# A fixed vector-engine order, pairs of tiles and ScalarE roots in the opening stage of a graph layer

## The chip, the cores and the metric

The kernel runs on one core of a Trainium2 chip. The time is the device time of one execution in microseconds (us). Nine executions of the kernel before took 1905.69 to 1914.63 us, with a median of 1910.33 us. A separate execution was profiled; all lines of the profile come from that one.

In the profile, PE is TensorE's matmul unit and PEld its weight load, DVE is VectorE, ACT is ScalarE, POOL is GpSimd and SP is SyncE, which here only starts transfers. Each engine works through a queue of instructions in the order in which they stand there; a semaphore makes an instruction wait for another engine.

## The reference, cut to what matters

The layer normalises 3125 nodes of 256 features and sends the result through a graph network (GNN) and through a transformer with linear attention of depth 4; the sum of both goes through a mixture of experts.

```python
xn = _layernorm(x, axis=-1)
x = x + _L0_gnn_ref(xn, edge_attr_3, src, dst, ...) + _L0_mix_ref(xn[None], ...)[0]
x = x + _L0_ffn_ref(_layernorm(x, axis=-1)[None], ...)[0]
...
# in _L0_gnn_ref: 100000 edges
m = jnp.concatenate([h[edge_src], w], axis=1)
tmp = jax.nn.relu(m @ W1.T + b1)
h_N = jax.ops.segment_sum(tmp, edge_dst, num_segments=h.shape[0])
...
# in _L0_mix_ref, for each of 4 layers
h = _layernorm(x, ln1_g[i], ln1_b[i])
x = x + _linear_attn(h, Wq[i], Wk[i], Wv[i], Wo[i], bo[i])
h = _layernorm(x, ln2_g[i], ln2_b[i])
x = x + (jax.nn.gelu(h @ W1[i] + b1[i], approximate=False) @ W2[i] + b2[i])
...
# in _linear_attn, with 8 heads of 32
q = jax.nn.softmax(split(x @ Wq) * scale, axis=-1)
k = jax.nn.softmax(split(x @ Wk) * scale, axis=-2)
context = jnp.einsum('bhnd,bhne->bhde', k, v)
out = jnp.einsum('bhnd,bhde->bhne', q, context)
```

The part of the graph network that is the same for all edges of a source node, `xn @ W1[:, :256].T`, is computed once for each node; it is called `proj` here and lies in a table in DRAM, from which each edge gathers its row.

## The kernel before

The nodes stand in 25 tiles of 125 rows (partitions). Tiles are worked through in seven blocks (`BLOCKS`): five of four tiles, one of three, one of two. `pairs(b)` cuts a block into pairs of tiles, since two tiles of 256 columns fill one PSUM buffer of 512 columns; seven such buffers (`mm_tile`) go round.

The opening stage, which makes xn, proj and the attention inputs of layer 0, is a chain for each block b:

- `stage_xn` (L478 to L495): DVE takes the statistics of each tile (`bn_stats`, `bn_aggr`, L91 and L92) and from them two inverse roots for each row: that of the first normalisation and that of the second, which layer 0's attention applies to the normalised rows. Three small instructions (L488 to L490) make both arguments, `rsqrt` (L108 to L116) finds both roots at once by an integer first guess and three Newton steps, eleven small instructions. L493 normalises the tiles in place in `xm`, L495 makes the scale of the second normalisation.
- `stage_xnT`: PE transposes the normalised tiles (L238), ACT copies them out of PSUM (L509), SP stores them to DRAM for later (L510).
- `stage_xh1`: ACT multiplies by the second scale (L499).
- `stage_proj`: PE multiplies by `W1h` (L519), ACT copies (L521), SP writes the rows of the proj table.
- `stage_t1`: PE transposes the rows of `stage_xh1`, and ACT (L459) and DVE (L461), a half each, apply gain and bias: `hT`.
- `stage_k`: PE computes the k products of the block (L552), DVE takes their maximum over the nodes (L554), `neg` and, from block 1 on, `alpha` (L559, L567), ACT takes the exponentials (L563).
- `stage_q`: for each pair PE computes q products (L576), DVE takes the maximum of each head and subtracts it (L587, L588), ACT takes the exponentials (L589), DVE divides by the sum (L595 to L597).
- `stage_m`, `stage_ek`, `stage_qT`: the product of k and rows summed over nodes (L629, with DVE's L632 or L634), and transposes.

The loop over blocks (L817 to L844) does k, q of block b, m of block b-1, then xnT, xh1, proj and t1 of block b+1, then ek and qT of block b. `stage_xn(b + 2)` stands in it right after `stage_k(0, b)`. `windows` is a generator that prepares the sums of edges: it finds, from the sorted destinations `dst_i`, the first node of each strip of edges (DVE: L305, L308, L315, L319; two transposes on PE for each quarter, L314 and L318). The loop calls `next(prepared)` between its stages from block 2 on.

The order of work within an engine: `manual_schedule(engines=in_order)` (L808) keeps PE, ACT and POOL in the order of the program text. DVE isn't in that set in the opening stage: there a scheduler chooses DVE's order from its own estimates. Later, around `context` and `stage_y`, DVE is in program order as well (L848).

POOL clears the table `hNT` (two halves of 3157 columns) at the start, in one instruction (L273); the table collects the sums of messages, to which DVE adds windows from L370 on. POOL also makes the identity mask `ident`, which all transposes use, and starts the gathers of proj rows (L348), each group behind a tiny copy (`tick`, L436) that waits until a named tile is written.

Of the kernel before, what the change touches and what calls it, by code (L numbers as in the profile page):

```python
# [39 lines left out]
BT = 4  # L40
# [25 lines left out]
def gps_layer(ctx: ExitStack, tc: tile.TileContext, a, out):  # L66
    nc = tc.nc

    def cols(t0, n=1):
        return slice(t0 * TP, (t0 + n) * TP)  # L70
# [149 lines left out]
    with ExitStack() as ph:  # L220
# [49 lines left out]
        w1w = edge.tile([P, SC * D], F32, name="w1w", bufs=1)  # L270
        proj = dram.tile([N, D], F32, name="proj")
        xnT_d = dram.tile([P, KC, N], F32, name="xnT_d")
        nc.gpsimd.memset(hNT, 0.0)  # L273


        xv = by_tile(a["x"])
# [198 lines left out]

        def stage_xn(b):  # L478
            r = BLOCKS[b]
            n = len(r)  # L480
            for t in r:
                stats(tmp, xm[:, t, :], t)
            rs = tmp.tile([TP, 3, 2, BT], F32, name="rs", bufs=3)
            st["rs", b] = rs
            v = mv[:, r[0]:r[-1] + 1, 1]
            if n < BT:
                nc.vector.memset(rs[:, 0], 1.0)
            nc.vector.tensor_scalar(rs[:, 0, 0, :n], v, EPS, None, op0=ALU.add)  # L488
            nc.vector.scalar_tensor_tensor(rs[:, 0, 1, :n], rs[:, 0, 0, :n], EPS, v, op0=ALU.mult, op1=ALU.add)
            nc.vector.tensor_mul(rs[:, 0, 1, :n], rs[:, 0, 1, :n], rs[:, 0, 0, :n])  # L490
            rsqrt(rs[:, 1], rs[:, 0], rs[:, 2])
            for i, t in enumerate(r):
                nc.vector.tensor_scalar(xm[:, t, :], xm[:, t, :], mv[:, t, 0:1], rs[:, 1, 0, i:i + 1],  # L493
                                        op0=ALU.subtract, op1=ALU.mult)
            nc.vector.tensor_mul(rs[:, 2, 0, :], rs[:, 0, 0, :], rs[:, 1, 1, :])  # L495

        def stage_xh1(b):
            for i, t in enumerate(BLOCKS[b]):
                nc.scalar.activation(xh1s[b % 2][:, i, :D], xm[:, t, :], AF.Copy,  # L499
                                     scale=st["rs", b][:, 2, 0, i:i + 1])  # L500

        def stage_xnT(b):
            r = BLOCKS[b]
            xnT = stage0[:, b % 2 * KC * BT * TP:(b % 2 + 1) * KC * BT * TP].rearrange(
                "p (c m) -> p c m", c=KC)
            st["xnT", b] = xnT
            for t0, o, n in pairs(b):
                ps = transposed(xm[:, t0:t0 + n, :], n, "xnT_ps")
                nc.scalar.copy(xnT[:, :, cols(o, n)], ps)  # L509
            nc.sync.dma_start(xnT_d[:, :, cols(r[0], len(r))], xnT[:, :, :len(r) * TP])  # L510

        def stage_proj(b):
            r = BLOCKS[b]
            pj = pjs[b % 2]
            for t0, o, n in pairs(b):
                pp = mm_tile("proj_ps")[:TP].rearrange("p (i d) -> p i d", d=D)
                for i in range(n):
                    for c in range(KC):
                        nc.tensor.matmul(pp[:, i, :], st["xnT", b][:, c, cols(o + i)], w1h[:, c, :],  # L519
                                         start=(c == 0), stop=(c == KC - 1))  # L520
                nc.scalar.copy(pj[:, o:o + n, :], pp[:, :n, :])  # L521
            by_parts(nc.sync, by_tile(proj)[:, r[0]:r[-1] + 1, :], pj[:, :len(r), :])


        def stage_stats(b):
# [7 lines left out]
            for i, t in enumerate(r):  # L533
                normalize(xh1[:, i, :D], xm[:, t, :], t)

        def stage_t1(l, b):
            hT = tmp.tile([P, KC, BT * TP], F32, tag="hT", name="hT", bufs=2)
            st["hT", b] = hT
            for t0, o, n in pairs(b):
                ps = transposed(xh1s[b % 2][:, o:o + n, :D], n, "hT_ps")  # L540
                affine(hT[:, :, cols(o, n)], ps, l, 0)
                worked(n * KC * P, hT[:1, 1, o * TP:o * TP + 1])
# [55 lines left out]

        def stage_q(l, b):
            st["qs", b] = tmp.tile([TP, BT, D], F32, name="qs")  # L600
            for pair in pairs(b):
                qf, qm = q_exp(b, pair, q_products(b, pair))
                q_shares(pair, qf)
                worked(pair[2] * KC * D, qm[:1, :1])
# [203 lines left out]
        with tc.manual_schedule(engines=in_order):  # L808

            prepared = windows()  # L810
            stage_xn(0)
            stage_xnT(0)
            stage_xh1(0)
            stage_proj(0)
            stage_xn(1)
            stage_t1(0, 0)
            for b in range(NB):  # L817
                stage_k(0, b)
                if b + 2 < NB:
                    stage_xn(b + 2)  # L820
                if b < NB - 1:
                    stage_q(0, b)
                else:
                    held = True
                if b > 1:
                    next(prepared, None)
                if b > 0:
                    stage_m(0, b - 1)
                if b + 1 < NB:
                    stage_xnT(b + 1)  # L830
                    stage_xh1(b + 1)
                    if b > 1:
                        next(prepared, None)
                    stage_proj(b + 1)
                    stage_t1(0, b + 1)
                if b > 1:
                    next(prepared, None)
                stage_ek(0, b)
                if b < NB - 2:
                    stage_qT(0, b)  # L840
                if b == NB - 2:
                    for _ in prepared:
                        pass
                    spread = True  # L844
            stage_m(0, NB - 1)
            for l in range(last):
                start_layer(l)
                with tc.manual_schedule(engines={mybir.EngineType.DVE}):  # L848
                    if l == 0:
                        context(l, [lambda: stage_qT(l, NB - 2, slice(0, 1)),  # L850
                                    lambda: stage_qT(l, NB - 2, slice(1, 2)), lambda: None])
                    else:
                        context(l, [lambda: None, lambda: None, rest])
                    load(l + 1, "Wk", "Wq", "Wv")
                    (y00, y01), (y10, y11), (y20, y21) = [pairs(b) for b in range(3)]
                    y_added(*y_products(y00))
                    held, only_loads = False, True
                    y_added(*y_products(y01))
                    stage_ln2(0, None)
                    y10, y11 = y_products(y10), y_products(y11)  # L860
                    stage_qT(l, NB - 1)
                    y20 = y_products(y20)
                    y_added(*y10)
                    stage_t2(l, 0)
                    y21 = y_products(y21)
                    for y in (y11, y20, y21):
                        y_added(*y)
                    only_loads = False
                for b in range(NB):
                    stage_f1(l, b)  # L870
                    if b == 0:
                        add_b2(b)
                    if b > 1:
                        stage_ek(l + 1, b - 2)
                        stage_qT(l + 1, b - 2)
                    if 1 < b < NB - 1:
                        stage_y(l, b + 1)
                    if b > 1:
                        stage_m(l + 1, b - 2)
                    if b > 0:  # L880
                        stage_t1(l + 1, b - 1)
                    if b + 1 < NB:
                        stage_ln2(b + 1)
                    stage_f2(l, b)
                    stage_stats(b)
                    if b == NB - 1:
                        stage_ln1(b)
                        held = True
                        fill(2)
                    if b > 0:  # L890
                        stage_k(l + 1, b - 1)
                    if b + 1 < NB:
                        stage_t2(l, b + 1)
                    if b > 0:
                        stage_q(l + 1, b - 1)
                    if b < NB - 1:
                        stage_ln1(b)
                stage_ek(l + 1, NB - 2)
                stage_t1(l + 1, NB - 1)
                stage_m(l + 1, NB - 2, [0])  # L900
                stage_k(l + 1, NB - 1)
                stage_m(l + 1, NB - 2, [1])
                stage_qT(l + 1, NB - 2)
                stage_ek(l + 1, NB - 1)
                rest = fill_win()
                if l + 1 == last:
                    rest()
                stage_m(l + 1, NB - 1)
            while due:
                _, _, step, i = due.pop()  # L910
                step(i)
# [586 lines left out]
```

## Time and profile before

| what | value |
|---|---|
| median of nine executions | 1910.33 us |
| the profiled execution: its time | 1907.14 us |
| the profiled execution: its span | 1905.4 us |
| PE busy, 0 to 20 us and 20 to 40 us | 9.63 us, 14.06 us |
| PE busy, 40 to 60, 60 to 80, 80 to 100, 100 to 120 us | 19.76, 19.87, 19.84, 19.66 us |
| granted clock of PE, whole span | 0.976 |
| first k product of block 0, 1, 2, 3, 4 | 18.96, 43.85, 61.54, 79.34, 97.25 us |
| first gather of proj rows | 132.56 us |

Times within the execution count from the start of its span. The span leaves out what lies around it (1.7 us here). A row of the timeline holds the start, the length, the engine, the line, the operation, the tile that is written and those that are read, their sizes, the number of instructions merged, and, in square brackets, how long the engine had been idle and what released it. The granted clock is the share of its full clock that PE was given.

The opening stage in the order of PE's work: block 0's transposes begin at 9.63 us and its proj at 11.46; the k products of block 0 begin at 18.96, wait 3.62 us for the second half of `hT` and go on from 23.68; block 1's proj begins at 36.02. From about 40 us on PE has no gaps of more than 0.3 us until block 3's end.

### The profile page before, as it was taken

The numbers are of one execution on the slowest core, as the hardware profiler recorded it, in microseconds if no ns is written. First come the engines' busy times: TensorE is split into PE (matmuls) and PEld (weight loads), VectorE is DVE, ScalarE is ACT, GpSimd is POOL, SyncE is SP. The second block draws the span as 40 slices with busy tenths as digits, with TensorE's granted clock in tenths as the row PEclk, the third lists the DMA queues.
The fourth block names the chain that finished last, engine by engine and source line by source line (L and its number), as shares of the span: only waits on it lengthen the run. The fifth ranks groups of instructions, "written<-read, shape, count | busy, mean of one in ns | idle before, by whom it ended". The sixth has DMA issues, their size and how long they took to land. (4 is left out here: it accounts for less than half of the span.)

```text
span 1905.4 us, 28580 instructions
## 1 busy us (share of the span) xinstructions
PE 1796.4 (94%) x8965; PEld 1217.4 (64%) x8965; DVE 1161.6 (61%) x3729; ACT 746.0 (39%) x1352; POOL 1110.2 (58%) x1404
## 2 busy tenths in 40 slices
PE   6999899999989999999899999999999999999975
PEld 4875555666655565566665656656677777788752
DVE  8656576756774666666666667666555665433326
ACT  3543354444524544554334445444222222222213
POOL 1006788788828888888468788881123337555521
PEclk8999999999989999999999999999999998999997
DMA  6212333333523333334323333332221004677836
GB/s 164 95 63 81 95 110 100 99 103 103 152 67 92 103 101 102 109 103 128 114 68 107 95 105 103 104 105 76 86 70 31 20 17 123 209 277 269 282 121 196
DMA packets 95089, 216.64 MB, mean 114 GB/s; under 512 B 26761, under 2 KB 53392, under 8 KB 90193
## 3 DMA queue, kind: packets, MB, share of 16 engines
q0 software_dynamic: 45904, 121.36, 22.3%
q1 hardware_dynamic: 49024, 93.34, 15.4%
q8 instruction: 77, 1.26, 0.3%
q14 instruction: 84, 0.68, 0.1%
HBM read 192.20 MB, written 22.35 MB: 113 GB/s over the span
## 5 line engine op out<-in xcount | busy, mean ns | idle before, releaser
L348 POOL DMA_INDIRECT gat<-proj,src_i x784 | 760.4, 970 | 192.4 <-issue 144.9
L735 PE MATMUL f_ps<-h2T,ww 128*128 128x500 f32 (+2 forms) x896 | 360.6, 550 | 6.9 <-ACT h2T L459 6.2
L745 PE MATMUL f_ps<-ww,gT 128*125 128x256 f32 x1600 | 363.3, 382 | 0.0
L398 ACT ACTIVATE gat<-gat 128x512 f32<-128x512 f32 x392 | 238.6, 630 | 305.2 <-DVE gat L397 299.5
L397 DVE TENSOR_TENSOR gat<-gat,pw 128x512 f32<-128x512 f32 x392 | 250.3, 677 | 160.8 <-PE pw L392 141.3
L745 PEld LDWEIGHTS f_ps<-ww,gT 128*125 128x125 f32 x1600 | 294.1, 188 | 70.4 <-issue 18.2
L735 PEld LDWEIGHTS f_ps<-h2T,ww 128*128 128x128 f32 x896 | 166.5, 192 | 178.7 <-issue 125.9
L737 ACT ACTIVATE gT<-f_ps,ffb 128x500 f32<-128x500 f32 (+2 forms) x224 | 135.3, 631 | 134.9 <-PE f_ps L735 134.6
L378 PE MATMUL pq<-gat,hot 128*32 128x256 f32 x1568 | 131.5, 390 | 10.1 <-ACT gat L398 8.8
L370 DVE TENSOR_TENSOR hNT<-hNT,win_ps 128x64 f32 x392 | 84.5, 215 | 64.9 <-PE win_ps L367 54.4
L392 PE MATMUL pw<-w1w,ea 8*128 8x512 f32 x784 | 119.3, 639 | 0.5 <-ACT gT L737 0.3
L750 DVE TENSOR_TENSOR xm<-xm,f_ps 125x512 f32<-125x512 f32 (+1 forms) x52 | 34.7, 667 | 138.0 <-PE f_ps L745 130.6
L1201 POOL DMA_INDIRECT slots<-rec,at x50 | 59.4, 1189 | 101.0 <-DVE rs_u L115 63.8
L576 PE MATMUL q_ps<-wwq,hT 128*125 128x256 f32 x400 | 97.1, 394 | 6.8 <-DVE gat L397 5.0
L629 PE MATMUL m_ps<-xh,ek 125*128 125x257 f32 x400 | 95.6, 389 | 5.7 <-ACT ek L615 5.7
L211 POOL DMA_INDIRECT outs<-o,ids x50 | 49.3, 986 | 87.9 <-DVE o L209 86.9
L552 PE MATMUL k_ps<-hT,wwk 128*128 128x500 f32 (+2 forms) x224 | 94.6, 566 | 4.4 <-DVE hT L461 3.6
L204 PE MATMUL e_ps<-ew,hs 128*128 128x256 f32 x400 | 97.2, 380 | 0.5 <-DVE o L208 0.3
L688 PE MATMUL y_ps<-mo,qT 128*125 128x256 f32 x400 | 92.6, 382 | 3.4 <-DVE mo L678 3.4
L576 PEld LDWEIGHTS q_ps<-wwq,hT 128*125 128x125 f32 x400 | 75.8, 194 | 28.4 <-DVE gat L397 8.6
L91 DVE BATCH_NORM_STATS2 bnst<-xm 125x6 f32<-125x256 f32 x225 | 89.6, 413 | 4.6 <-DMA xm<-x 2.4
L629 PEld LDWEIGHTS m_ps<-xh,ek 125*128 125x128 f32 x400 | 76.2, 194 | 20.3 <-ACT ek L615 7.2
(270 smaller groups left out, 2546.1 us busy)
## 6 DMA issues: line engine op xcount, KB each, us to landing
ew<-ffn_w SPq DMA_DIRECT2D x33, 1154.0 KB
gat<-proj,src_i POOLq DMA_INDIRECT x784
ww<-mix_W SPq DMA_DIRECT2D x8, 1024.0 KB
ea<-ea_g SPq DMA_DIRECT2D x98, 64.0 KB
hNT<-ffn_w SPq DMA_DIRECT2D x4, 1154.0 KB
ogs<-outs SPq DMA_DIRECT2D x10, 448.0 KB
xnT_d<-stage SPq DMA_DIRECT2D x5, 500.0 KB
xnT<-xnT_d SPq DMA_DIRECT2D x5, 500.0 KB
```

Source lines behind the costliest of these rows:

```text
L204: nc.tensor.matmul(ps[:, j, :], x["hs"][:, f, j * P:(j + 1) * P], x["w2"][:, f, :], start=(f == 0), stop=(f == NEF - 1))
L348: nc.gpsimd.indirect_dma_start(out=gats[-1][:, (j // SC) % 2, j % SC, :], out_offset=None, in_=proj, in_offset=bass.IndirectOffsetOnAxis(a ...
L378: nc.tensor.matmul(pq[s * W:(s + 1) * W, :], hot[:, s * SC + i, :], gats[s // 2][:, s % 2, i, :], start=(i == 0), stop=(i == SC - 1))
L392: nc.tensor.matmul(pws[s], ea[s * W:s * W + SC * 4, :], w1w[s * W:s * W + SC * 4, :], start=True, stop=True)
L397: nc.vector.tensor_add(msg, msg, pws[s])
L398: nc.scalar.activation(msg, msg, AF.Relu)
L552: nc.tensor.matmul(ps, wt["Wk"][:, h, c * P:(c + 1) * P], hT[:, h, :m], start=(h == 0), stop=(h == KC - 1))
L576: nc.tensor.matmul(ps[:, i, :], st["hT", b][:, c, cols(o + i)], wt["Wq"][:, c, :], start=(c == 0), stop=(c == KC - 1))
L629: nc.tensor.matmul(ps, st["ek", b][:, i, c * P:(c + 1) * P], xh1s[b % 2][:, i, :], start=(i == 0), stop=(i == n - 1))
L735: nc.tensor.matmul(ps, wt["W1"][:, c, f * P:(f + 1) * P], st["h2T", b][:, c, :m], start=(c == 0), stop=(c == KC - 1))
L737: nc.scalar.activation(gT[:, f, :m], ps, AF.Gelu, bias=ffb[:, l, f:f + 1])
L745: nc.tensor.matmul(ps[:, i, :], st["gT", b][:, f, cols(o + i)], wt["W2"][:, f, :], start=(f == 0), stop=(f == NF - 1))
```

## The change

DVE joins the engines in program order from the start of the opening stage to its end (`prologue`). The stages of block 0, and `stage_xn` of block 1, are cut into pairs of tiles, and the calls for the pairs are interleaved by hand. For these two blocks ACT's `Sqrt` and DVE's `reciprocal` take the place of the integer guess and Newton steps; all other blocks keep `rsqrt`. In layer 0, `stage_q` does products, subtraction and exponential of both pairs first, and then the divisions of both. The clearing of `hNT` is cut into four pieces, each on POOL behind a tick on `hT` of blocks 1 to 4.

```diff
-        nc.gpsimd.memset(hNT, 0.0)
...
-        def stage_xn(b):
+        def stage_xn(b, part=None):
+
             r = BLOCKS[b]
-            n = len(r)
-            for t in r:
+            o, n = (0, len(r)) if part is None else pairs(b)[part][1:]
+            tt = slice(r[0] + o, r[0] + o + n)
+            for t in range(tt.start, tt.stop):
                 stats(tmp, xm[:, t, :], t)
...
-            rsqrt(rs[:, 1], rs[:, 0], rs[:, 2])
...
+            v, rv, ru, rw = mv[:, tt, 1], *[rs[:, k, :, o:o + n] for k in range(3)]
+            nc.vector.tensor_scalar(rv[:, 0], v, EPS, None, op0=ALU.add)
+            nc.vector.scalar_tensor_tensor(rv[:, 1], rv[:, 0], EPS, v, op0=ALU.mult, op1=ALU.add)
+            nc.vector.tensor_mul(rv[:, 1], rv[:, 1], rv[:, 0])
+            if part is None:
+                rsqrt(ru, rv, rw)
+            else:
+                nc.scalar.activation(rw, rv, AF.Sqrt)
+                nc.vector.reciprocal(ru, rw)
...
         def stage_q(l, b):
             st["qs", b] = tmp.tile([TP, BT, D], F32, name="qs")
+            if l == 0:
+                for pair, qf in [(pair, q_exp(b, pair, q_products(b, pair))[0]) for pair in pairs(b)]:
+                    q_shares(pair, qf)
+                return
...
             prepared = windows()
-            stage_xn(0)
-            stage_xnT(0)
-            stage_xh1(0)
-            stage_proj(0)
-            stage_xn(1)
-            stage_t1(0, 0)
+            prologue = ExitStack()
+            prologue.enter_context(tc.manual_schedule(engines={mybir.EngineType.DVE}))
+            one, two = slice(0, 1), slice(1, None)
+            stage_xn(0, 0)
+            stage_xnT(0, one)
+            stage_xn(0, 1)
+            stage_xh1(0, one)
+            stage_proj(0, one)
+            stage_xnT(0, two)
+            stage_xn(1, 0)
+            stage_t1(0, 0, one)
+            stage_xh1(0, two)
+            stage_proj(0, two)
+            stage_t1(0, 0, two)
+            stage_xn(1, 1)
             for b in range(NB):
                 stage_k(0, b)
                 if b + 2 < NB:
...
                     stage_proj(b + 1)
                     stage_t1(0, b + 1)
+                    if b < 4:
+                        nc.gpsimd.tensor_copy(tick, st["hT", b + 1][:1, 0, :1])
+                        nc.gpsimd.memset(hNT[:, b % 2, b // 2 * N // 2:(b // 2 + 1) * N // 2 + b // 2 * W], 0.0)
...
             stage_m(0, NB - 1)
+            prologue.close()
```

`stage_xnT`, `stage_xh1`, `stage_proj` and `stage_t1` take the pair as an argument, too; the transfers of `stage_xnT` and `stage_proj` are issued once, with a block's last pair.

## The prediction

> **What bounds the kernel now.** I read the busy shares first, then stretches of 20 us, then the order of time from 10 to 80 us, then the granted clock in steps of 1 us.
>
> ```profile
> PE 1796.4 (94%) x8965; PEld 1217.4 (64%) x8965; DVE 1161.6 (61%) x3729; ACT 746.0 (39%) x1352; POOL 1110.2 (58%) x1404
> ...
> 20.00:40.00 20.00, 14.06 (x42) 9.40 (x42) 17.32 (x74) 5.57 (x11) 0.00 (x0) 0.74 0.35 111
> ...
> 60.00:80.00 20.00, 19.87 (x108) 16.08 (x107) 14.77 (x47) 11.55 (x25) 0.00 (x0) 1.00 0.23 77
> ```
>
> PE is busy 94% of the span, so time is won only where PE stands still or slow. Columns of a stretch: length, then busy us of PE, PEld, DVE, ACT, POOL, then the granted clock. From 0 to 40 us PE works 23.7 us, so up to 16 us are open. From 40 us on, in the attention blocks of layer 0, PE is full: blocks 1 to 3 start their k products at 43.85, 61.54, 79.34 us, 17.7 us apart. There a new wait costs its full length. One such block, start and length in us:
>
> ```profile
> 61.54 3.52 PE L552 MATMUL k_ps<-hT,wwk 128*128 128x500 f32 x8
> ...
> 66.08 0.15 DVE L567 TENSOR_TENSOR alpha<-kmax,kmax 128x2 f32<-128x2 f32 x1
> ...
> 66.83 0.69 DVE L587 TENSOR_REDUCE qm<-q_ps 125x16 f32<-125x512 f32 x1 [0.59 <-PE q_ps L576]
> ...
> 69.75 0.68 DVE L588 TENSOR_TENSOR qs<-q_ps,qm 125x512 f32<-125x512 f32 x1
> ...
> 70.47 0.63 ACT L589 ACTIVATE qs<-qs 125x512 f32<-125x512 f32 x1 [1.50 <-DVE qs L588]
> ...
> 72.46 1.05 ACT L509 COPY stage<-xnT_ps 128x500 f32<-128x500 f32 x2 [1.36 <-PE xnT_ps L238]
> ...
> 73.09 3.72 PE L519 MATMUL proj_ps<-w1h,stage 128*125 128x256 f32 x16
> ```
>
> The reader is to see a chain: DVE's second subtract of q (69.75) releases ACT's second exp; ACT, in a fixed order, copies xnT only behind it; PE's proj needs that copy. Here ACT waits 1.36 us for PE, so the chain has that much slack. It has it because DVE, whose order a scheduler chose, goes from alpha straight to q; the normalisation of block b+2 was done in idle DVE time before.
>
> **The change, part by part.** All is summed on the profiled span (1905.4 us; that execution took 1907.14; the median shown is 1910.33, 4.9 above the span) and the difference is added to the median.
>
> *Clearing hNT.* One POOL memset of 5.36 us (6314 columns) becomes four of 1562 or 1595 columns, by columns 1.33 to 1.35 us each, each behind a 0.18 us tick. POOL is idle 124.7 us before its tick at 131.45, and DVE first adds to hNT at 178.07: cost 0. Were that cover gone, 6 us would lie before the first gather (132.56). The next write of hT in that buffer must wait for the tick, two blocks later: 0. The identity mask, behind the memset at 6.37, is free about 5 us sooner, which the earlier transposes below need.
>
> *Block 0 in pairs, roots on ACT.* The Newton steps L110 to L116 are 11 instructions 0.20 us apart, 2.2 us; a Sqrt and a reciprocal take their place, by the nearest small rows (ACT alpha 0.20, DVE reciprocal 0.24) 0.5 us with hand-over. Two tiles: statistics from 4.00 to 5.15, three small ops to 5.72, root and reciprocal to 6.2, tile 0 normalised at 6.6. PE starts there, 3.0 us before the 9.63 of now. From there ACT's and PE's orders decide: proj of the first pair, at the slow 0.46 us per matmul that the first eight show now (3.7 us), from 8.45 to 12.15; the second pair's copy to 13.7; block 1's first root stands behind that copy, so DVE idles from 11.8 to 13.95; proj of the second pair ends 16.3 (2.15 us, as the second eight now) to 17.8 (slow again); the last half of hT is written at 18.0 to 19.6, against 23.63 now. Block 1's second half then takes DVE 3.0 us, the two k reductions and neg 1.5: neg at 22.5 to 24.0, against 29.85 now. So 6 to 7 us are won here. Block 0's DMAs (three) are the same; SP now issues an ea load and a 1 MB weight ahead of block 1's proj, which only the gather at 132.56 waits for: 0.
>
> The Trainium skill (ScalarE: Activation LUTs, What ACT_TABLE_LOAD costs) asks about 2.7 us for each change of table set and tells to do all of one set first, which speaks against roots in a kernel of exps. In this trace a load takes 1283 ns. The built order has one more load, behind the last root and ahead of the first exp, where ACT waits some 2 us for neg anyway: 0 by the row; by the page at most 0.7 us.
>
> *DVE in program order.* Now neg is followed by all of stage_xn(b+2), and only then by q. Its price: statistics in strict alternation as in layer 0's y stage, 0.56 us per tile and 0.64 for the last (148.55, 149.11, 149.75), 2.32; from L488 to the next stage 12.27 to 16.45, 4.18; together 6.5 us for four tiles. These rows are of the same instructions:
>
> ```profile
> 12.27 0.17 DVE L488 TENSOR_SCALAR rs<-mv 125x4 f32<-125x4 f32 x1
> ...
> 15.08 1.38 DVE L493 TENSOR_SCALAR xm<-xm,mv,rs 125x256 f32<-125x256 f32 x4
> ...
> 16.38 0.15 DVE L495 TENSOR_TENSOR rs<-rs 125x4 f32<-125x4 f32 x1
> 16.45 0.74 DVE L91 BATCH_NORM_STATS2 bnst<-xm 125x6 f32<-125x256 f32 x2
> ```
>
> Queued behind it on DVE is q, behind q's exps on ACT the copy of xnT(b+1), behind that PE's proj. Block 1, in us from its k: alpha 4.54, xn 4.62 to 11.1; maximum, subtract, maximum, subtract start 11.1, 11.82, 12.42, 13.14 (0.72 and 0.60 apart as in the rows; both subtracts now come before the sums, which saves 0.88 against now), the last ends 13.82; exp to 14.49; copy, 0.63 later proj at 15.1 where it now is at 11.55: **+3.55**. PE has finished m and xnT at 11.3 and idles 3.8.
> Block 2: the first part of the windows (L305 0.56, L308 0.96), which the scheduler had put at 21.15, now follows the last share of q (16.30): done at 18.5. PE's least transpose stands between xnT and proj and waits for it: proj at 18.6, **+7.05**.
> Block 3: three tiles (5.7 us), last share at 15.5, then lcol, for which PE's base transpose waits ahead of proj: 16.6 for 11.66, **+4.9**.
> Block 4: two tiles (4.8 us), proj at 13.4 for 11.66, **+1.7**. Blocks 5 and 6 have no such stage: 0. Sum 17.2 us.
> Block 0 likewise: from neg, xn(2) and q hold proj(1) until 32.9 to 34.4, against 36.02. So of the 6 to 7 us only 1.6 to 3.1 reach proj(1).
>
> *The clock.* An idle PE is followed by slow matmuls (length, PE busy, granted clock, DMA share, GB/s):
>
> ```profile
> 21.00:22.00 1.00, 0.00 (x0) 1.00 0.57 172
> 22.00:23.00 1.00, 0.00 (x0) 0.88 0.22 41
> 23.00:24.00 1.00, 0.32 (x1) 0.50 0.49 134
> ...
> 29.00:30.00 1.00, 1.00 (x5) 0.70 0.00 0
> ```
>
> Three stalls of now: 3.6 us before 23.68, then 6.0 us at half clock; 2.3 us before 36.02, 3.4 us; 5.5 us before 202.47, 4.7 us. Half of that is lost: 3.0, 1.7, 2.4, mean 2.4. Blocks 1 to 3 idle 3.8, 7.2 and 5.0 us: 2.4 each, 7.2 together, bounds 0 and 3 x 3.0 = 9. Block 4 idles 1.9, less than any of the three: 0 (1.7 as a bound). Block 0's stall, 7 us, pays 2.4 too, where now it pays 1.7: k(1) comes 0.9 to 2.4 earlier, taken 1.7.
> The Trainium skill (TensorE: Matmul & The Clock Gate, What's actually happening) gives free-running windows of about 3.4 us: one idle window halves the clock, a busy one restores it. The drops here last about 3.4 and 6.8 us, as it says, but the 2.3 us gap also dropped the clock, which its "at least one idle window" would spare; by the page alone block 1's stall would drop it only where it meets a window whole, and the sum would be about 2 us lower.
>
> *After the prologue* DVE's scheduler orders block 1 of the first feed-forward a little differently. PE waits 5.46 us there for a gather that POOL, saturated since 149 us, issues; that shifts with everything else: 0, bounds -2.4 and +2.4 (one clock drop).
>
> **Sum:** 17.2 + 7.2 - 1.7 = +22.7 us; on the median 1933.0. Least: 17.2 + 0 - 2.4 - 2.4 = +12.4, 1923; most: 17.2 + 9 + 1.7 + 2.4 - 0.9 = +29.4, 1940.
>
> **The rivals.**
> *The stalls come, the clock holds.* +15.5, 1926. For it: at 142 to 144 us PE was idle 1.9 us and the clock stayed 1.00. Against: the three drops above. It lies inside my bounds.
> *DVE keeps up; faster.* One mechanism: DVE gets through xn(b+2) so quickly that q's second subtract ends by 10.3 us after k (8.9 now, plus the slack of 1.36), so that ACT again waits for PE. That takes a stage of 3.0 us instead of 6.5. There it is about even: proj(1) at 29.6 to 31.1 wins 4.9 to 6.4, and the windows' ops in blocks 2 and 3 still cost 3.5 and 1.4. It decides below 3.0; with 1.0 us block 0 wins 7.7 and block 2 loses 1.5, -6.2: 1904. For it: the small ops are busy only 0.17 of 0.20 us. Against: the four L493 alone take 1.38 and four statistics 1.5.
> *The edit isn't what it says:* in the built programs DVE stands in program order up to block 5, so this falls.
> *Worse:* clock drops as long as the 10 us from 1606 to 1616, and the scheduler's new order costs too: +35, 1945.
>
> **How the numbers follow.** Forecast with its clock variants 0.80, its own range 1923 to 1940; faster 0.11; a stage near the 3.0 us, that is no change, 0.03; worse 0.06. About 0.2% (3.8 us) is what can be told from no change here. The range goes down to 1917 for a stall partly hidden and to 1942. Faster 0.11, same 0.03, slower 0.86.
>
> **What would show it.** Right: k(0)'s neg near 23 us; ACT's xnT copies behind a wait for DVE's qs instead of PE; PE idle 3 to 7 us ahead of proj in blocks 1, 2 and 3, the longest in block 2 at the least transpose; these blocks 23 to 28 us long; clock 0.5 in them. Wrong: blocks still 17.7 us apart, or a first block that saves over 10 us at k(1).

## The result, and the profile after

The changed kernel is slower: 1928.39 us (median of 13 executions, 1923.37 to 1934.38) against 1910.28 us (40 executions of the kernel before); the ratio is 1.0101, 95% interval 1.0090 to 1.0111. Its profiled span is 1931.5 us, granted clock 0.97, against 1905.4 and 0.976. Chips differ: the kernel before takes 1903.7 to 1904.7 us on those of nine runs below, and 2164.5 us, at a granted clock of 0.923 to 0.935, on that of three (Newton steps, the table cleared first, q in pairs alone). So each run is given as a ratio to the kernel before on its own chip, and of those three only the first 120 us of the trace are compared.

The table compares k products, at which blocks begin (us from the start of the span). Below, k(1) is the first k product of block 1, and so on; mo is the product of the output weights and the context, which follows the attention blocks of a layer.

| first k product of block | 0 | 1 | 2 | 3 | 4 | 5 |
|---|---|---|---|---|---|---|
| before | 18.96 | 43.85 | 61.54 | 79.34 | 97.25 | 114.08 |
| after | 16.28 | 39.50 | 62.30 | 89.98 | 114.70 | 133.15 |
| difference | -2.68 | -4.35 | +0.76 | +10.64 | +17.45 | +19.07 |

Block 0 wins 4.35 us; blocks 1 to 4 lose 5.11, 9.88, 6.81 and 1.62. At the first mo product +18.4 us is left of it, close to the difference of the medians (18.1). First the busy shares of the changed kernel's page, then its stretches (length, busy us of PE, PEld, DVE, ACT, POOL, granted clock, DMA share, GB/s):

```profile
PE 1804.4 (93%) x8965; PEld 1223.0 (63%) x8965; DVE 1170.1 (61%) x3719; ACT 748.2 (39%) x1357; POOL 1114.1 (58%) x1411
...
60.00:80.00 20.00, 13.61 (x71) 10.58 (x69) 14.85 (x46) 8.46 (x18) 1.62 (x3) 0.91 0.14 49
...
100.00:120.00 20.00, 15.01 (x70) 11.47 (x69) 10.59 (x27) 8.45 (x17) 1.54 (x2) 0.83 0.15 52
```

Over the span PE's share hardly moves, 94 to 93%; in the stretch from 60 to 80 us PE works 13.61 us where it worked 19.87. Block 2 in order of time, from the timelines of PE, DVE and ACT (start, length, engine; in brackets the idle time before and what ended it):

```profile
62.30 3.52 PE L563 MATMUL k_ps<-hT,wwk 128*128 128x500 f32 x8
...
66.91 0.42 DVE L91 BATCH_NORM_STATS2 bnst<-xm 125x6 f32<-125x256 f32 x1
...
73.28 0.15 DVE L502 TENSOR_TENSOR rs<-rs 125x4 f32<-125x4 f32 x1
...
75.39 0.69 DVE L599 TENSOR_TENSOR qs<-q_ps,qm 125x512 f32<-125x512 f32 x1
...
76.11 0.63 ACT L600 ACTIVATE qs<-qs 125x512 f32<-125x512 f32 x1 [0.63 <-DVE qs L599]
76.65 1.03 ACT L517 COPY stage<-xnT_ps 128x500 f32<-128x500 f32 x2
...
79.81 0.97 DVE L307 TENSOR_REDUCE least<-drel 128x392 f32<-128x784 f32 x1
...
80.92 0.42 PE L313 MATMUL least_ps<-ident,least 128*98 128x128 f32 x1 [7.32 <-DVE least L307]
81.14 6.31 PE L528 MATMUL proj_ps<-w1h,stage 128*125 128x256 f32 x16
```

From 66.91 to 73.35 us DVE does all of `stage_xn(4)`; only then q, whose second subtract ends at 76.1 us; ACT's copy of xnT follows the second exp without a gap, where before it waited 1.36 us for PE. The windows' minimum (79.81) is later still, and PE's small transpose needs it: idle for 7.32 us. Then proj takes 6.31 us instead of 3.72. The waits of PE up to 140 us, in total, number and longest:

```profile
PE proj_ps L528 <- ACT stage L517: 13.8, 5, 7.2
PE least_ps L313 <- DVE least L307: 7.3, 1, 7.3
...
PE base_ps L317 <- DVE lcol L314: 5.0, 1, 5.0
```

### The profile page after: what moved, and what is told of

The parts are those of the page before. It is cut to its first block, busy times and chain, and to the rows that moved or that the text cites. A ratio compares the mean times of both kernels' runs of the same rounds, so it can differ in the third digit from the quotient of the medians.

```text
span 1931.5 us, 28587 instructions
## 1 busy us (share of the span) xinstructions
PE 1804.4 (93%) x8965; PEld 1223.0 (63%) x8965; DVE 1170.1 (61%) x3719; ACT 748.2 (39%) x1357; POOL 1114.1 (58%) x1411
## 5 line engine op out<-in xcount | busy, mean ns | idle before, releaser
L760 PEld LDWEIGHTS f_ps<-ww,gT 128*125 128x125 f32 x1600 | 293.8, 188 | 71.3 <-issue 18.4
L703 PEld LDWEIGHTS y_ps<-mo,qT 128*125 128x125 f32 x400 | 75.1, 193 | 21.8 <-DVE mo L693 5.0
```

Source lines behind the costliest of these rows:

```text
L703: nc.tensor.matmul(ps[:, i, :], qT[:, c, cols(t0 + i)], mo[:, c, :], start=(c == 0), stop=(c == KC - 1))
L760: nc.tensor.matmul(ps[:, i, :], st["gT", b][:, f, cols(o + i)], wt["W2"][:, f, :], start=(f == 0), stop=(f == NF - 1))
```

## Experiments

First a table of all runs, with the length of each block in us, from its first k product to the next block's; then the single ones.

| run | block 0 | 1 | 2 | 3 | 4 | ratio to before |
|---|---|---|---|---|---|---|
| before | 24.89 | 17.69 | 17.80 | 17.91 | 16.83 | 1 |
| after | 23.22 | 22.80 | 27.68 | 24.72 | 18.45 | 1.0101 (1.0090 to 1.0111) |
| loop left to the scheduler | 15.88 | 17.94 | 18.76 | 17.98 | 16.84 | 0.9963 (0.9950 to 0.9975) |
| fixed order alone | 26.28 | 25.21 | 29.50 | 27.33 | 23.32 | 1.0165 (1.0151 to 1.0178) |
| after, xn behind q | 15.85 | 23.20 | 19.23 | 18.21 | 18.39 | 0.9998 (0.9987 to 1.0009) |
| after, long fillers | 24.10 | 23.67 | 30.79 | 27.17 | 20.12 | 1.0161 (1.0148 to 1.0174) |
| after, short fillers | 24.08 | 21.11 | 24.89 | 22.72 | 20.11 | 1.0071 (1.0057 to 1.0086) |
| after, windows early | 24.03 | 23.88 | 24.01 | 24.73 | 18.45 | 1.0081 (1.0067 to 1.0094) |
| after, q as before | 26.50 | 25.16 | 29.49 | 27.31 | 23.30 | 1.0160 (1.0146 to 1.0174) |
| after, no fixed order | 16.73 | 17.69 | 19.46 | 17.98 | 16.83 | 0.9991 (0.9981 to 1.0000) |
| loop free, Newton roots | 16.96 | 17.69 | 18.76 | 17.98 | 16.84 | 0.9994 (0.9971 to 1.0017) |
| loop free, table cleared first | 17.53 | 17.69 | 17.80 | 17.91 | 16.84 | 0.9972 (0.9938 to 1.0005) |
| before, q in pairs | 23.19 | 17.70 | 17.80 | 17.91 | 16.83 | 0.9989 (0.9963 to 1.0014) |
| loop free, pieces late | 15.87 | 17.69 | 17.81 | 17.90 | 16.84 | 0.9956 (0.9942 to 0.9969) |

### The loop left to the scheduler

```diff
             stage_xn(1, 1)
+            prologue.close()
             for b in range(NB):
...
             stage_m(0, NB - 1)
-            prologue.close()
```

> The changed kernel, but DVE is in fixed order only up to the last call ahead of the loop over blocks; inside the loop the scheduler orders it again. Theory (the loss is xn(b+2) standing ahead of q in the fixed order, and the pairs, roots and pieces by themselves help or cost nothing): the four stalls of 3.7, 7.3, 5.0 and 1.9 us go, blocks 1 to 4 come back to 17.0 to 17.9 us each, and block 0 keeps at least the 4.4 us that k(1) now gains over the kernel before, more if q is no longer held up: k(1) at 32 to 39 us, time 1897 to 1906. Rival 1 (the pairs, the roots or the pieces on POOL cost something in the blocks): blocks stay over 18.5 us, time 1912 to 1928. Rival 2 (the gain at block 0 is lost again behind it): blocks 17.8 us, but the first mo product not earlier than the 141.4 us of the kernel before, time 1908 to 1913.

0.9963: some 7 us faster than before, 26 us faster than the change. Blocks 1 to 4 are back at 16.8 to 18.8 us, and k(1) comes at 32.94 us, 10.9 earlier than before (up to 2.8 of it by PE's clock, as the run with q in pairs alone shows) and 6.6 earlier than in the changed kernel. So the loss comes with the fixed order inside the loop. What remains of PE's waits there, from PE's timeline of this run:

```profile
26.79 3.72 PE L528 MATMUL proj_ps<-w1h,stage 128*125 128x256 f32 x16 [1.80 <-ACT stage L517]
...
69.64 3.59 PE L563 MATMUL k_ps<-hT,wwk 128*128 128x500 f32 x8 [0.80 <-DVE hT L460]
```

With q right behind neg, proj(1) waits 1.80 us instead of 7.21 and runs at full clock. The second row, a wait of 0.80 us that makes block 2 0.96 us longer than before, is taken up with the last run.

### The fixed order alone

```diff
             prepared = windows()
+            prologue = ExitStack()
+            prologue.enter_context(tc.manual_schedule(engines={mybir.EngineType.DVE}))
             stage_xn(0)
...
             stage_m(0, NB - 1)
+            prologue.close()
```

> The kernel before with one thing added: DVE in program order over the opening stage. No pairs, Newton steps for all blocks, the table cleared at the start, q as before. Theory: blocks 1 to 4 are longer by what they are in the changed kernel, 5.1, 9.9, 6.8 and 1.6 us (block 1 by up to 0.9 more, since the sums of the first pair of q now stand ahead of the second subtract); block 0 is 1 to 3 us shorter than before, since hT no longer waits behind other rows; time 1927 to 1934. Rival (pairs, roots or pieces carry a part of the loss): the blocks are longer by less than 15 us together, time 1912 to 1922.

1.0165, 31 us, more than the theory allowed, and far from the rival. Blocks 1 to 4 are 2.4, 1.8, 2.6 and 4.9 us longer than in the changed kernel, and block 0, expected 1 to 3 us shorter than before, is 1.4 us longer. Block 1 of this run, DVE's and PE's timeline:

```profile
55.94 0.69 DVE L588 TENSOR_TENSOR qs<-q_ps,qm 125x512 f32<-125x512 f32 x1
57.38 0.69 DVE L595 TENSOR_REDUCE qr<-qs 125x16 f32<-125x512 f32 x1 [0.76 <-ACT qs L589]
...
59.72 0.69 DVE L588 TENSOR_TENSOR qs<-q_ps,qm 125x512 f32<-125x512 f32 x1
...
61.59 5.36 PE L519 MATMUL proj_ps<-w1h,stage 128*125 128x256 f32 x16 [6.11 <-ACT stage L509]
```

In the order of the text DVE waits 0.76 us for ACT's first exp, divides (1.6 us), and only then takes the second pair's maximum and subtract: the second subtract starts 3.78 us behind the first, 1.32 in the changed kernel (74.07 and 75.39). The next run asks whether this is what the other edits of the change made up for.

### q as before

```diff
-            if l == 0:
-                for pair, qf in [(pair, q_exp(b, pair, q_products(b, pair))[0]) for pair in pairs(b)]:
-                    q_shares(pair, qf)
-                return
             for pair in pairs(b):
```

> The changed kernel with stage_q as before: shares of the first pair ahead of the products' subtract of the second. Theory from the run with the fixed order alone, whose blocks 1 to 4 were 2.4, 1.8, 2.6 and 4.9 us longer than the changed kernel's: DVE waits 0.7 us for the first exp and does 1.6 us of shares before the second subtract, so q ends 2.4 us later in each block 0 to 4; the first k product of block 5 comes 12 to 15 us later than at 133.15 us, 1.0160 to 1.0180 times the kernel before. Rival (the pairs of block 0 and the roots account for most of the difference between the two kernels): k of block 5 at most 6 us later, 1.010 to 1.0135.

1.0160; k(5) comes at 148.67 us, 15.5 later than in the changed kernel, 0.5 over the expected range (0.6 us of it stand already at k(0), ahead of any q); the theory holds and the rival falls. Blocks 1 to 4 are those of the fixed order alone to 0.05 us. In block 4 the wait ahead of proj grows from 1.93 to 4.39 us, and proj behind it takes 5.28 us instead of 2.85; hence 4.9 us there. So the small edit to q was worth more, with DVE in a fixed order, than all the others together: without it the whole change costs 1.60%, and the fixed order alone 1.65%. k(1) comes at 43.41, only 0.44 earlier than before: pairs and roots bring almost nothing there while q stands behind xn(2) and its own divisions.

### q in pairs alone

```diff
             st["qs", b] = tmp.tile([TP, BT, D], F32, name="qs")
+            if l == 0:
+                for pair, qf in [(pair, q_exp(b, pair, q_products(b, pair))[0]) for pair in pairs(b)]:
+                    q_shares(pair, qf)
+                return
             for pair in pairs(b):
```

> The kernel before with the layer 0 order of q alone: products, subtract and exp of both pairs, then both divisions; DVE left to the scheduler. Theory (this order matters only where DVE is held to the text, since the scheduler puts the second subtract ahead of the divisions anyway): k(1) to k(5) within 1 us of 43.85 and 114.08, 0.999 to 1.001 times the kernel before. Rival (the order of q carries the gain of the kernel with a free loop): k(1) 2 us or more earlier, 0.995 to 0.9985.

The time (0.9963 to 1.0014) decides nothing on that chip. Blocks 1 to 4 stay within 0.01 us of the kernel before: with a scheduler the edit has no effect on them, as the theory said. But k(1) comes 2.8 us earlier, which it excluded. No wait of PE accounts for that: its wait for hT ends at 23.69 as before (23.68), and the one ahead of proj lasts 2.32 us as before (2.33). Behind them the rest of k, q and proj take 4.61, 3.62 and 3.72 us instead of 5.37, 3.99 and 5.41: the granted clock is 1.00 while proj runs (35 to 38 us), where it was 0.50 before (37 to 39 us). So the 2.8 us are where the slow clock fell in one execution of each kernel, and no shorter wait. Lengths of block 0 in the table carry a scatter of that size.

### xn behind q, still in a fixed order

`stage_xs` is the loop over `stats` taken out of `stage_xn` for the later blocks.

```diff
+                if 0 < b < NB - 2:
+                    stage_xs(b + 2)
                 stage_k(0, b)
-                if b + 2 < NB:
-                    stage_xn(b + 2)
                 if b < NB - 1:
                     stage_q(0, b)
...
+                if b == 0:
+                    stage_xs(2)
-                if b > 1:
+                if b > 2:
                     next(prepared, None)
                 if b > 0:
                     stage_m(0, b - 1)
+                if b + 2 < NB:
+                    stage_xn(b + 2)
+                if b == 1:
+                    next(prepared)
```

> The changed kernel with DVE still in fixed order, but the order is another: from block 1 on the statistics of block b+2 stand ahead of the k reductions, where DVE waits 2.2 us for PE, and the rest of stage_xn(b+2) behind q and m; in block 0 all of stage_xn(2) stands behind q; the first windows part is in block 1. Theory (not the fixed order, but the place of stage_xn in it costs): ACT's copy of xnT again waits for PE, no stall over 1 us ahead of proj in blocks 2 to 5, block 1 at most 1.5 us longer than before, k(1) at 34 to 37 us, time 1899 to 1907. Rival (any fixed order costs, since DVE has 16 to 17 us of work in a block of 17.7): stalls ahead of the k products of 1 to 3 us in each of blocks 2 to 4, time 1908 to 1918.

0.9998, no difference to the kernel before, some 20 us better than the change. The stalls of 3.7 to 7.3 us ahead of proj are gone, so most of the loss is the place of `stage_xn`, with the windows' first part, and not a fixed order as such. The rest of the theory was too hopeful: block 1 lasts 23.20 us, because xn(2) now stands ahead of DVE's half of hT(1), so that PE waits 3.54 us within the k products and then works slowly. DVE's, POOL's and PE's timelines of this run:

```profile
31.98 1.45 DVE L111 TENSOR_SCALAR rs<-rs 125x8 int32<-125x8 int32 x1
31.98 1.39 POOL L873 MEMSET hNT<- 128x1562 f32 x1
...
36.64 0.98 DVE L460 TENSOR_SCALAR hT<-hT_ps,lnp 128x250 f32<-128x250 f32 x2
37.67 4.48 PE L568 MATMUL k_ps<-hT,wwk 128*128 128x500 f32 x6 [3.54 <-DVE hT L460]
```

The first row, one small instruction of xn(2) that takes 0.17 us elsewhere, lasts 1.45 us beside POOL's first piece, and DVE has no idle time from there to hT: 1.3 of the 3.54 us are this, which the last two runs take up. Blocks 2 to 4 keep 0.3 to 1.6 us. k(5) comes 7.7 us later than under the scheduler, and the time is 0.35% (6 to 7 us) behind that run, on the same chip. The figure of 1899 to 1907 us, which the run met, was reckoned against a slower chip.

### Idle matmuls that keep PE busy

```diff
+        KEEP = {1: 15, 2: 31, 3: 21}
...
+        def stage_keep(b):
+            ps = mm_tile("keep_ps")
+            for i in range(KEEP.get(b, 0)):
+                nc.tensor.matmul(ps[:, :D], w1h[:, i % KC, :P], w1h[:, i % KC, :], start=True, stop=True)
...
                     stage_xh1(b + 1)
+                    if b in KEEP:
+                        stage_keep(b)
```

> The changed kernel with idle matmuls (15, 31 and 21 of 256 columns, into a PSUM buffer that nobody reads) on PE between xnT and proj of blocks 1, 2 and 3, some 3.4, 7.0 and 4.8 us at full clock, which fill the stalls but do not outlast them by more than 0.3 us. Theory (the idling PE loses its clock): the proj matmuls behind them take 3.7 to 3.9 us instead of 5.41, 6.31 and 5.55, the granted clock stays 1.00 from 44 to 115 us, and k(4) comes 5.5 to 6.5 us earlier than at 114.70; time 1920 to 1924. Rival (the slow proj has another cause, such as its operands): proj stays over 5 us, time 1927 to 1931.

1.0161. Each matmul of the program is two rows of the trace, so the fillers lasted 6.6, 13.6 and 9.3 us, twice what was meant, and delayed proj themselves; the time says nothing about the clock. But proj behind them took 3.6 us in all three blocks. The second run has 8, 16 and 10:

> As the run with 15, 31 and 21 idle matmuls, but with 8, 16 and 10: each was two rows in the trace and lasted 0.44 us, so the fillers had outlasted the stalls by 3, 6 and 4 us, while the proj behind them took 3.6 us each. Now they last 3.5, 7.0 and 4.4 us and end 0.2 to 0.5 us before the data. Theory (an idle PE loses its clock): proj of blocks 1, 2 and 3 takes 3.6 to 3.8 us (5.41, 6.31, 5.55 in the changed kernel), blocks 1 to 3 last 21.0 to 21.4, 24.8 to 25.2 and 22.8 to 23.3 us (22.80, 27.68, 24.72), and the kernel is 5 to 7 us faster than the changed kernel: 1.0065 to 1.0075 times the kernel before. Rival (the slow proj costs no time in the end, since other work waits anyway): same block lengths as the changed kernel, 1.0095 to 1.011.

1.0071, about 5.7 us better than the change. PE's timeline of this run:

```profile
52.13 3.62 PE L525 MATMUL keep_ps<-w1h 128*128 128x256 f32 x16
55.96 3.72 PE L534 MATMUL proj_ps<-w1h,stage 128*125 128x256 f32 x16 [0.20 <-ACT stage L518]
...
73.24 7.08 PE L525 MATMUL keep_ps<-w1h 128*128 128x256 f32 x32
80.72 0.29 PE L313 MATMUL least_ps<-ident,least 128*98 128x128 f32 x1 [0.40 <-DVE least L307]
80.84 3.62 PE L534 MATMUL proj_ps<-w1h,stage 128*125 128x256 f32 x16
```

proj starts as late after k as in the changed kernel (14.97 us in block 1 in both), but runs at full speed. Blocks 1, 2 and 3 are shorter by 1.69, 2.79 and 2.00 us, 6.5 us together: that is the share of the clock, shown as time. Block 4, without a filler, lasts 20.11 us in this run and 18.45 in the changed kernel: there proj took 4.54 us instead of 2.85, after the same 1.93 us of idling.

### The windows' first part early

```diff
-                if b > 1:
+                if b > 2:
                     next(prepared, None)
                 if b > 0:
                     stage_m(0, b - 1)
+                if b == 1:
+                    next(prepared)
```

> The changed kernel with the first part of the windows (the cast and the minimum of the destinations, 0.56 and 0.96 us on DVE) moved from block 2 to block 1, behind m, where DVE idles 3.8 us. Theory (PE's least transpose, and proj behind it, wait for these two, as well as for q's shares in front of them): block 2 comes down from 27.68 us to 22.6 to 23.2, the length of block 1, its stall from 7.3 to 3.7 us; block 3 stays 24 to 25 us, since base there waits for lcol; 1.0070 to 1.0082 times the kernel before. Rival (DVE is late in block 2 whatever it does): block 2 26 us or more, 1.0095 to 1.011.

1.0081. In PE's timeline the transpose of least no longer waits, and proj of block 2 does, for ACT's copy, as in block 1:

```profile
55.88 6.50 PE L528 MATMUL proj_ps<-w1h,stage 128*125 128x256 f32 x16 [3.65 <-ACT stage L517]
...
79.78 6.50 PE L528 MATMUL proj_ps<-w1h,stage 128*125 128x256 f32 x16 [3.55 <-ACT stage L517]
...
105.22 0.43 PE L317 MATMUL base_ps<-ident,lcol 98*128 98x98 f32 x1 [4.99 <-DVE lcol L314]
```

The stall of block 2 falls from 7.32 to 3.55 us, as the theory has it; block 3 keeps its 4.99. Block 2 is 3.67 us shorter, not 4.5 to 5.1, since proj there lasts 6.50 us: the same idle time of 3.65 us made proj of block 1 last 6.50 us here and 5.41 in the changed kernel.

### No fixed order at all

```diff
             prologue = ExitStack()
-            prologue.enter_context(tc.manual_schedule(engines={mybir.EngineType.DVE}))
```

> The changed kernel without any fixed order for DVE in the opening stage; pairs, roots, q and pieces as changed. Theory (the gain of the run with the loop left to the scheduler comes from pairs and roots): blocks 1 to 4 17 to 18.8 us each, k(1) at 32 to 36 us, 0.996 to 0.999 times the kernel before. Rival (the gain needs the fixed order of the first calls, since the scheduler lets later statistics and norms in ahead of what PE waits for): k(1) at 38 us or later, 0.999 to 1.002.

0.9991, just above the theory's range. k(1) comes at 34.61 us, as the theory has it, and k(5) at 106.57, 7.5 us earlier than before; so in the opening stage pairs and roots carry most of the gain, and fixing the first calls adds 0.8 us at the first transposes (6.89 for 7.66) and 1.7 at k(1). By time it is otherwise: the gain is about 2 us of the 7 of the run with the free loop. Part of the 7.5 us is gone where this profile begins layer 1's k products (-5.8 us), and at the last mo product 2.8 us are left. What takes it was not tried and stays open. Block 2, 19.46 us, is longer than the theory allowed; there DVE's normalisation at 69.51 us lasts 1.65 us instead of 0.40, beside POOL's piece at 69.60.

### Newton steps in the first two blocks

```diff
-            if part is None:
-                rsqrt(ru, rv, rw)
-            else:
-                nc.scalar.activation(rw, rv, AF.Sqrt)
-                nc.vector.reciprocal(ru, rw)
+            rsqrt(ru, rv, rw)
```

> The kernel with the loop left to the scheduler (0.9963 times the kernel before), with one thing put back: Newton steps instead of ACT's Sqrt and DVE's reciprocal in the first two blocks. Theory (a root costs DVE 1.8 us less by Sqrt, and the chain of block 0 is DVE's): the first transposes come 1.7 to 2.0 us later than at 6.89, k(1) 2 to 5 us later than at 32.94, 0.9973 to 0.9990 times the kernel before. Rival (the pairs alone give the gain, the roots are hidden behind PE and ACT): k(1) within 1 us of 32.94, 0.995 to 0.9972.

From the first statistics to the first transposes 4.51 us pass, against 2.77 with Sqrt: 1.74 more, as expected. k(1) comes 1.85 us later, just short of the expected 2 (2.15 later, counted from the first statistics), and k(5) 1.6 later. The time itself (0.9971 to 1.0017) can't confirm so little on that chip.

### The table cleared first

```diff
+        nc.gpsimd.memset(hNT, 0.0)
...
-                    if b < 4:
-                        nc.gpsimd.tensor_copy(tick, st["hT", b + 1][:1, 0, :1])
-                        nc.gpsimd.memset(hNT[:, b % 2, b // 2 * N // 2:(b // 2 + 1) * N // 2 + b // 2 * W], 0.0)
```

> The kernel with the loop left to the scheduler, with the table of the sums cleared at the start in one piece as before. Theory (the move of the clearing costs and wins nothing): in the kernel before the identity mask is ready at 6.65 us, and the first transposes now start at 6.89, so they stay within 0.2 us; 0.995 to 0.9975 times the kernel before. Rival (the pieces in the loop, or the ticks in front of them, cost, or the mask's delay does): k(1) or a later block moves by over 1 us either way, below 0.995 or above 0.9978.

Here the rival holds by the trace, while the time (0.9938 to 1.0005) decides nothing. The first transposes come 3.94 us after the first statistics (2.77 in the run with the free loop), and k(1) 2.7 us later; blocks 1 to 3 are 0.25, 0.96 and 0.07 us shorter. POOL's and DVE's timelines of this run:

```profile
0.96 5.37 POOL L273 MEMSET hNT<- 128x6314 f32 x1
...
4.50 0.40 DVE L91 BATCH_NORM_STATS2 bnst<-xm 125x6 f32<-125x256 f32 x1
...
5.14 1.21 DVE L491 TENSOR_SCALAR rs<-mv 125x2 f32<-125x2 f32 x1
6.38 0.29 DVE L492 SCALAR_TENSOR_TENSOR rs<-rs,mv 125x2 f32<-125x2 f32 x1
```

The mask was not what was late. DVE's small instruction on SBUF, 0.17 us elsewhere, lasts 1.21 us and ends when POOL's memset ends (6.33 us). That is 1.2 of the 2.7 us at k(1). Another 1.34 us PE waits within k(0) for a half of hT, ahead of which the scheduler had put the windows' cast and minimum (18.47 and 19.07 us); whether the clearing led it to that order isn't shown.

### The pieces later

```diff
-                    if b < 4:
+                    for i in {3: (0, 1), 4: (2,), 5: (3,)}.get(b, ()):
                         nc.gpsimd.tensor_copy(tick, st["hT", b + 1][:1, 0, :1])
-                        nc.gpsimd.memset(hNT[:, b % 2, b // 2 * N // 2:(b // 2 + 1) * N // 2 + b // 2 * W], 0.0)
+                        nc.gpsimd.memset(hNT[:, i % 2, i // 2 * N // 2:(i // 2 + 1) * N // 2 + i // 2 * W], 0.0)
```

> The kernel with the loop left to the scheduler, with the four pieces of the clearing moved from blocks 0 to 3 to blocks 3 (two), 4 and 5, where DVE has no normalisation left (its last is at 70.35 us there). In the run before, the piece that POOL started at 67.48 us ended at 68.90, and DVE's normalisation that started at 67.40 took 1.65 us instead of 0.40 and hT behind it came late, so that PE waited 0.80 us ahead of k in block 3. Theory (POOL's memset held DVE up): that row takes 0.35 to 0.45 us, the wait of PE ahead of k(3) goes, block 2 lasts 17.8 to 18.0 us instead of 18.76; the time changes by less than can be measured, 0.9945 to 0.9970 times the kernel before. Rival (DVE was late for another reason): block 2 stays at 18.5 to 18.8 us.

First the run with the free loop, DVE's and POOL's timelines, then this run, DVE's:

```profile
67.40 1.65 DVE L500 TENSOR_SCALAR xm<-xm,mv,rs 125x256 f32<-125x256 f32 x1
...
67.48 1.42 POOL L863 MEMSET hNT<- 128x1595 f32 x1
...
68.97 0.96 DVE L460 TENSOR_SCALAR hT<-hT_ps,lnp 128x250 f32<-128x250 f32 x2
```

```profile
67.04 0.41 DVE L500 TENSOR_SCALAR xm<-xm,mv,rs 125x256 f32<-125x256 f32 x1
67.37 0.98 DVE L460 TENSOR_SCALAR hT<-hT_ps,lnp 128x250 f32<-128x250 f32 x2
```

The normalisation takes 0.41 us instead of 1.65, hT is written 1.6 us earlier (0.4 of it from the blocks ahead), PE's wait is gone and block 2 lasts 17.81 us: the theory, to the row; DVE's order is the same in both kernels. By time the two can't be told apart (0.9963 and 0.9956). By its blocks this is the best version, and it is faster than both kernels: 7 to 8 us below the one before.

## Why the prediction was right or wrong

The forecast, 1933.0 us with the stalls of blocks 1 to 4 as its mechanism, was right in sign and mechanism and 4.6 us high. Of these, 3.6 us stand at k(5) already.

- *DVE in program order, 17.2 us.* Right block by block. proj was put at 15.1, 18.6, 16.6 and 13.4 us after k in blocks 1 to 4; it stands at 14.97, 18.84, 16.64 and 13.25. That a stage of 6.5 us ahead of q is the cause is shown by the two runs that take it from there (the loop left to the scheduler, and xn behind q); that block 2 also pays for the windows is shown by moving these (7.32 to 3.55 us).
- *The clock, 7.2 us.* The run with short fillers showed 6.5 us. In the run with early windows block 1, whose stall is as long (3.65 us), lost 1.1 us more, so the sum over three stalls varies from one execution to the next.
- *Together*, 24.4 us were put on blocks 1 to 4, and 23.4 were lost.
- *Block 0, 1.7 us won.* This term was mis-sized: 4.35 us in the two profiled executions. The first transposes (6.6; measured 6.77) and the start of proj of the first pair (8.45; 8.60) were right, but the last half of hT was put at 18.0 to 19.6 and was written at 16.81, so neg came at 20.98 instead of 22.5 to 24.0. The working had proj of the second pair end at 16.3 to 17.8, and it ended at 15.14: proj of the first pair took 3.40 us and not 3.7, ACT's copy and the root behind it came 0.6 to 0.7 us sooner, and the second pair's products ran at full speed. This and the 1.0 us above are the 3.6 us between +22.7 and the +19.1 at k(5). Part of it is luck: in the three runs that do the same up to k(1), both with fillers and the one with early windows, k(1) comes at 40.92 to 41.02 us, 2.8 to 2.9 before the kernel before, and in the run with q in pairs alone block 0 ended 2.8 us sooner than in the kernel before by PE's clock alone.
- *q in pairs, 0.88 us saved.* The weakest price, though the sum hardly depended on it: it was read from rows that the scheduler had already interleaved. Under a fixed order the edit is worth 11.6 us in blocks 1 to 4, and 3.3 in block 0, where PE's wait ahead of proj(1) falls from 9.59 to 7.21 us and the rest is faster rows of PE.
- *Clearing hNT, 0.* Right for the changed kernel, whose DVE has no such instruction to do while POOL clears. But the reason given, POOL's idle time and the mask, missed what matters: POOL's memset holds DVE up. With the clearing first, the transposes come 1.2 us later; with pieces beside a free loop, block 2 loses 0.96 us.
- *The roots, 2.2 us to 0.5.* Right: 1.74 us on the first transposes. The table load (18.73 us, 1.28 us long) is hidden: ACT idles another 1.16 us behind it for neg. In the run with the free loop the first exp starts 2.05 us after the last root ends, the load and 0.76 us of waiting for neg included, so the 2.7 us that the prediction quotes as a price don't appear in this trace.
- *After the prologue, 0 within 2.4.* Right by the medians: PE's wait for the gather shrank from 5.46 to 3.97 us. The profiled execution loses 6.7 us more between the first and the last mo product, where both kernels do the same work; the run with early windows gains 3.5 there against the kernel before. This looks like scatter of single executions: the two profiled ones took 1933.23 and 1907.14 us, 4.8 above and 3.1 below their medians, and the medians agree with the +18.4 ahead of it; no run was made on it.
- *The rivals.* "DVE keeps up" fell by the stalls. "The clock holds" fell too, but not by the time: 1928.39 lies nearer to its 1926 than to 1933. What speaks against it is proj at 5.41, 6.31 and 5.55 us in blocks 1 to 3, and the 6.5 us that the short fillers won back.

## What to carry to other kernels

Fixing an engine's order pays where the next instruction is known to be on the path, here the first chain; in a loop where the engine is busy for three quarters of the time (DVE: 14.77 of 20 us before), write first what other engines wait for, or leave it to the scheduler. Price each reordering under the order that will hold after the change, not from rows that a scheduler has interleaved. And a transfer of work to an idle engine is free only if the two engines don't hold each other up: look for instructions that last longer than their like.

## What was unexpected in the hardware

DVE's `TENSOR_SCALAR` with all data in SBUF waits for a POOL memset: 0.17 became 1.21 us and 0.40 became 1.65 us, ending 0.02 and 0.15 us after the memset; statistics during the first kept their 0.40 us, and the two halves of hT, which DVE reads from PSUM, their 0.99 us beside a piece (38.20 us in the changed kernel). The Trainium skill (SBUF — State Buffer, Who interferes with whom) gives a reason: DVE and GpSimd share a pair of SBUF ports, held by one of them for a whole instruction, which DVE's two-port forms of `tensor_scalar` need. The rows agree, though they don't show which form ran; the prediction had not looked there.

The same idle time of PE costs different amounts. After 3.66 us of idling in block 1 the changed kernel's clock fell to half only at about 55.9 us, when proj had been running for 1.4 us, and came back 3.4 us later; after 3.65 us in the run with early windows it fell at about 54.7, while PE still idled, and came back 6.8 us later. These are rows in steps of 1 us, with length, PE busy, clock, DMA share and GB/s, first of the changed kernel, then of the run with early windows:

```profile
55.00:56.00 1.00, 1.00 (x6) 0.93 0.00 0
56.00:57.00 1.00, 1.00 (x4) 0.50 0.88 332
...
59.00:60.00 1.00, 1.00 (x7) 0.86 0.00 0
```

```profile
54.00:55.00 1.00, 0.00 (x0) 0.86 0.00 0
55.00:56.00 1.00, 0.12 (x1) 0.50 0.00 0
...
61.00:62.00 1.00, 1.00 (x4) 0.73 0.00 0
62.00:63.00 1.00, 1.00 (x10) 1.00 0.00 0
```

So the loss, 1.7 or 2.8 us, doesn't follow from the length of the idling alone; what else sets it wasn't tested. Block 4's 1.93 us show the same: no loss in the changed kernel, 1.7 us in the run with short fillers, the bound that the prediction had set.
